# Order of work in a fused convolution stage: opening tiles, a scale factor and a spectrum's mean change places

## The chip, the cores and the metric

The kernel runs on one core of one Trainium2 chip. TensorE (PE) does matrix products, VectorE (DVE) and ScalarE (ACT) elementwise work, GpSimd (POOL) elementwise work and DMA requests, SyncE (SP) DMA requests. PE writes its results to PSUM; the other data live in SBUF (on chip) and in device memory. The metric is the device time of one execution in microseconds, the median of several runs. In all data here the type is 32-bit float.

## The reference

The input x has shape 8 x 32 x 256 x 256 (batch, channel, height, width). Four layers follow one another, each of the form x + layer(groupnorm(x)), with 16 groups of two channels:

```
x = x + spectral(gn(x))      # rfft2, 32 x 32 low modes and 32 x 32 high modes mixed over channels, irfft2, bias
x = x + conv5x5(gn(x))       # one 5 x 5 kernel, the same for every channel, padding 2
x = x + gru(gn(x))           # a recurrence over the 256 columns
x = x + mix(gn(x))           # cumulative maxima in four directions, 1x1 mixing over 5*32 channels
```

Only the second half of the first layer (from modes back to the image) and the second layer matter here; both are in one stage.

## The kernel before

**Stages.** `forward_and_mix` computes the modes and mixes them over channels. `inverse_and_conv` transforms back, adds the input, and applies the convolution layer. `recurrence` and `maxima_and_mix` are the last two layers. The change is in `inverse_and_conv` alone, which is the stage from 355 to 1054 us of the profile.

**Tiling of the convolution stage.** There are 16 units `u`: a batch item and half of its channels (16), taken as two chunks `ch` of 8. A chunk has four groups `g` of two channels, so a unit has eight group convolutions, `g` from 0 to 7 in the main loop ("first" to "eighth group" in the text; `conv(u, g // G, g % G, between)`). The width is cut into nine blocks of 28 columns with a margin on each side; a block's transform is `transform(u, p)`, p from 0 to 8. Even units begin a batch item, odd ones end it.

**The order** is written out by hand (`manual_schedule`): every engine executes its instructions in the order in which the program emits them. One turn of the main loop emits a group convolution of unit u, then work for the next units: `transform(u + 1, p)` (one block; in the fourth group one more inside the convolution, `between`); in groups 4 to 7 `over_rows(u + 2, ...)`, which prepares the unit after next; at the eighth group `transform(u + 2, 0)`, "the lone transform", and `scale(u + 1, 0, 3)`.

**A group convolution** (`conv`, line 487) multiplies x by banded 64 x 64 matrices. Its result lies in three PSUM tiles, the banks: blocks 0 and 1 (first bank, 256 columns), blocks 2 to 5 (middle, 512), blocks 6 to 8 (last, 384). Each bank gets three kinds of tiles: kind 0 opens the accumulation, kinds 1 and 2 add to it, and each kind is a pair of 64 x 64 matmuls, one per half of the rows. The array has four 64 x 64 quadrants. A pair occupies two of them: the diagonal ones for kind 0 of the first and last bank and kinds 1 and 2 of the middle bank, the crossing ones for the rest. Pairs on different quadrants can run at the same time. Kind 0 and kind 1 of one bank lie on different quadrants but add to the same PSUM, so kind 1 waits for a semaphore that the bank's second opening matmul increments:

```
if kind == 1 and i == 0:
    ins._wait_ge(sems[bank], count[0])
```

The banks take turns in four PSUM buffers (`tag="vp", bufs=4`), three per convolution: the first bank gets the buffer that the last bank of the convolution before the previous one had, the middle bank that of the previous first bank, the last bank that of the previous middle bank.

**Eviction** (line 520): VectorE scales the PSUM results by r, adds x in place and sums, in five instructions: blocks 0, 1, then two for the middle bank, one for the last.

**Transform** (line 418, `up`; adds on line 427): 16 matmul passes in 64 x 32 tiles, then two VectorE additions. `over_rows` (line 401, `tp`) is preceding work, 8 passes, whose result ScalarE copies out of PSUM (line 408). **scale** (lines 451, 455, 457): PE sums squares (v), VectorE adds epsilon (ve), GpSimd takes the power -1/2 (r), which line 520 needs. The squares come from ScalarE (line 444). **spectrum** (lines 358 to 372): for a new batch item, one small matmul (y, line 360) and seven small VectorE operations fix the mean in the spectrum and write the group means. `over_rows`, `scale`, `spectrum` and `statistics` share one PSUM buffer, the tag "st". The spectrum is requested (`load_spectrum`) on ScalarE's queue in the third group of an odd unit; of the 8 batch items, the items 2 to 7 are prepared so, in units 1, 3, ..., 11. `store` requests the write of a finished chunk on SP's queue, after the fourth and eighth group; `load` requests the input on POOL's queue.

## Time and profile before

| what | value |
| --- | --- |
| median of 3 runs | 3101.18 us (3096.61 to 3104.53) |
| profiled execution | 3099.62 us, span 3097.8 us |
| PE busy, whole span | 2827.9 us (91%) |
| VectorE, ScalarE, POOL busy | 2584.2 (83%), 1868.6 (60%), 859.9 us (28%) |
| convolution stage, 355 to 1054 us | PE 683.9 of 699.0, VectorE 543.3, ScalarE 465.8 us; DMA engines 69% busy |
| convolution matmuls (line 487) | 4608 passes, 460.6 us busy |
| one eviction: 128, 384, 512 columns | about 0.35, 0.62, 0.75 us, and 0.08 us each to read the sum |

A profile row names the engine, the line of the kernel, the operation, and "output<-inputs" by the program's tile names: vp is the convolution's PSUM, up and tp that of the transforms, v that of scale, y that of spectrum, tt the copy of tp, junk the output of a sum of squares. PE is matmuls, PEld weight loads, which can overlap them. An f32 matmul appears as two passes, each with a weight load. "<-" with a name in a bracket or a list of waits is what ended an engine's idle time. The starts of single passes come from the single records of the trace; the ends of matmuls in it are modelled.

### The profile page before, as it was taken

The numbers are of one execution on the slowest core, as the hardware profiler recorded it, in microseconds if no ns is written. First come the engines' busy times: TensorE is split into PE (matmuls) and PEld (weight loads), VectorE is DVE, ScalarE is ACT, GpSimd is POOL, SyncE is SP. The second block draws the span as 40 slices with busy tenths as digits, with TensorE's granted clock in tenths as the row PEclk, the third lists the DMA queues.
The fourth block names the chain that finished last, engine by engine and source line by source line (L and its number), as shares of the span: only waits on it lengthen the run. The fifth ranks groups of instructions, "written<-read, shape, count | busy, mean of one in ns | idle before, by whom it ended". The sixth has DMA issues, their size and how long they took to land.

```text
span 3097.8 us, 111686 instructions
## 1 busy us (share of the span) xinstructions
PE 2827.9 (91%) x47736; PEld 1625.9 (52%) x47736; DVE 2584.2 (83%) x5178; ACT 1868.6 (60%) x4482; POOL 859.9 (28%) x1247
## 2 busy tenths in 40 slices
PE   7986799999999699999999999999999588888887
PEld 4656244444444366666666666666666333333333
DVE  5753577777777589999999999999999799999997
ACT  3332376667667678888888888888888222222222
POOL 0110011111111255555555555555555300000000
PEclk9985899999999899999999999999999799998998
DMA  9976577777775736656666656666664688888885
GB/s 385 389 278 210 161 226 213 211 210 219 210 215 175 179 91 160 165 143 143 143 150 165 161 142 143 144 155 165 152 146 115 192 319 328 330 322 328 326 327 228
DMA packets 468193, 655.69 MB, mean 212 GB/s; under 512 B 328784, under 2 KB 329696, under 8 KB 441456
## 3 DMA queue, kind: packets, MB, share of 16 engines
q1 hardware_dynamic: 407528, 487.89, 54.1%
q0 software_dynamic: 16784, 84.11, 8.2%
q10 hardware_dynamic: 43384, 76.55, 6.9%
q8 instruction: 374, 6.13, 0.8%
q14 instruction: 123, 1.01, 0.1%
HBM read 371.63 MB, written 272.63 MB: 208 GB/s over the span
## 4 chain that ended last, share of the span: by engine, by line
PE 71%; DVE 20%; DMA 3%; issue 3%; ACT 1%; SPq 0%; POOL 0%; ACTq 0%; DVEq 0%; POOLq 0%
PE vp L487 14%; PE r L753 14%; PE z L753 13%; PE ni L753 6%; PE nh L753 6%; PE up L418 4%; DVE rv L1012 4%; PE yp L131 3%; DVE dq L1018 2%; DVE uq L1020 2%; DVE m L1026 2%; DVE m L1022 2%; DVE m L1024 2%; PE tp L401 2%; PE o L1043 2%
## 5 line engine op out<-in xcount | busy, mean ns | idle before, releaser
L761 PE MATMUL z<-hs,weights 64*64 64x256 f32 x4080 | 539.3, 382 | 0.0
L761 PE MATMUL r<-hs,weights 64*64 64x256 f32 x4080 | 525.0, 375 | 0.0
L761 PE MATMUL ni<-hs,weights 64*64 64x256 f32 x4080 | 524.9, 375 | 0.0
L843 POOL TENSOR_TENSOR xw<-xw,hs 128x256 f32<-128x256 f32 x496 | 339.5, 685 | 635.6 <-DVE hs L842 635.6
L487 PE MATMUL vp<-x,c_conv 64*64 64x512 f32 (+5 forms) x4608 | 460.6, 495 | 4.3 <-DVE x L520 4.3
L1058 ACT ACTIVATE ot<-o,bres 128x512 f32<-128x512 f32 x256 | 154.9, 688 | 505.4 <-PE o L1043 490.0
L520 DVE SCALAR_TENSOR_TENSOR x<-vp,r,x 128x128 f32<-128x128 f32 (+2 forms) x640 | 350.4, 562 | 125.6 <-PE vp L487 106.7
L837 POOL TENSOR_TENSOR a<-zm,xn 128x256 f32<-128x256 f32 x510 | 372.4, 730 | 6.3 <-ACT zm L830 6.1
L835 ACT ACTIVATE n<-n,bih 128x256 f32<-128x256 f32 x510 | 259.2, 508 | 186.3 <-DVE n L834 186.3
L1043 PE MATMUL o<-m,wsc 32*32 32x512 f32 x3072 | 228.6, 724 | 108.1 <-DVE m L1026 104.5
L753 PE MATMUL r<-hs,weights 64*64 64x256 f32 x2040 | 319.1, 389 | 5.0 <-DVE hs L842 4.1
L487 PEld LDWEIGHTS vp<-x,c_conv 64*64 64x64 f32 x4608 | 201.9, 133 | 227.7 <-issue 107.1
L753 PE MATMUL z<-xn,weights 64*64 64x256 f32 x2040 | 305.5, 376 | 14.4 <-ACT xn L733 14.4
L753 PE MATMUL r<-xn,weights 64*64 64x256 f32 x2040 | 305.5, 376 | 1.2 <-ACT rs L828 1.2
L753 PE MATMUL nh<-xn,weights 64*64 64x256 f32 x2040 | 305.7, 377 | 0.0
L753 PE MATMUL z<-hs,weights 64*64 64x256 f32 x2040 | 305.2, 376 | 0.0
L753 PE MATMUL ni<-hs,weights 64*64 64x256 f32 x2040 | 305.2, 376 | 0.0
L733 ACT ACTIVATE xn<-xw,shift,turned 128x256 f32<-128x256 f32 x496 | 290.6, 586 | 0.0
L761 PEld LDWEIGHTS ni<-hs,weights 64*64 64x64 f32 x4080 | 284.5, 133 | 0.3
L829 DVE SCALAR_TENSOR_TENSOR n<-nh,bhh,rs 128x256 f32<-128x256 f32 x510 | 246.3, 483 | 45.9 <-ACT rs L828 31.4
L761 PEld LDWEIGHTS r<-hs,weights 64*64 64x64 f32 x4080 | 280.9, 131 | 0.2
L828 ACT ACTIVATE rs<-r,brz 128x256 f32<-128x256 f32 x510 | 241.3, 473 | 53.9 <-PE r L761 32.5
(162 smaller groups left out, 6233.8 us busy)
## 6 DMA issues: line engine op xcount, KB each, us to landing
xb<-in_xl_dram POOLq DMA_DIRECT2D x96, 768.0 KB, 6.3
xa<-in_xt_dram SPq DMA_DIRECT2D x64, 1024.0 KB
x<-x3d SPq DMA_DIRECT2D x32, 2048.0 KB
fw<-fwd SPq DMA_DIRECT2D x32, 2048.0 KB
out_dram<-ot ACTq DMA_DIRECT2D x64, 1024.0 KB
xw<-x2d SPq DMA_DIRECT2D x248, 256.0 KB
fwd<-fm SPq DMA_DIRECT2D x248, 256.0 KB
x3d<-xw SPq DMA_DIRECT2D x248, 256.0 KB
```

What stands on the lines that cost most here:

```text
L487: ins = nc.tensor.matmul(vps[bank][to, :, dst], lhsT=k.conv[r, P : P + 64] if kind == 2 else k.conv[r, o], rhs=pair_of(u, ch, g, lo, hi, s ...
L520: nc.vector.scalar_tensor_tensor(x, src[o], r1[rows, g : g + 1], x, ALU.mult, ALU.add, accum_out=s1[rows, 0, n, ch, g : g + 1])
L733: nc.scalar.activation(norms[bi][:, b, w], raws[bi][:, b, w], AF.Identity, bias=shift[:, b : b + 1], scale=sc[:, 1, b : b + 1])
L753: ins = nc.tensor.matmul(out[r], lhsT=weights[r, kind, gate, :], rhs=src[r], start=start, stop=stop)
L761: ins = nc.tensor.matmul(out[pairs[1 - i]], lhsT=weights[r, kind, gate, :], rhs=prev[r, :, q0 : q0 + Q], start=False, stop=stop,)
L828: rs = nc.scalar.activation(r, p["r"], AF.Sigmoid, bias=brz[:, 0:1])
L829: nc.vector.scalar_tensor_tensor(m, p["nh"], bhh[:, 2:3], r, ALU.add, ALU.mult)
L835: nc.scalar.activation(m, m, AF.Tanh, bias=bih[:, 2:3])
L837: product = nc.gpsimd.tensor_tensor(a, zm, cur, ALU.mult)
L843: nc.gpsimd.tensor_tensor(raw, raw, new, ALU.add)
L1043: nc.tensor.matmul(pts[b2][i][32 * j : 32 * j + 32].rearrange("p (w q) -> p w q", q=Q), lhsT=wsc[q, b2, t, :], rhs=src[j][q, b2], start=first,
L1058: nc.scalar.activation(ot[:, i], pts[b2][i], AF.Identity, bias=bres[:, b2, i : i + 1])
```

## The change

Three things in `inverse_and_conv` change places; no instruction is added or removed.

1. In `conv`, the first bank's opening tiles are emitted ahead of the middle bank's, in every group convolution.
2. In the eighth group, `scale(u + 1, 0, 3)` is emitted ahead of `transform(u + 2, 0)`.
3. In odd units, `spectrum` of the next batch item is emitted at the end of the sixth group, not of the eighth.

```diff
             count[0] += 1
-            for bank, kind in ((1, 0), (0, 0), (2, 0), (0, 1), (1, 1), (0, 2)):
+            for bank, kind in ((0, 0), (1, 0), (2, 0), (0, 1), (1, 1), (0, 2)):
                 tiles(bank, kind)
...
                     if g < len(PLACES) and more:
                         transform(u + 1, PLACES[g])
+                    if g == 2 * G - 1 and more:
+                        scale(u + 1, 0, 3)
                     if g == 2 * G - 1 and beyond:
                         transform(u + 2, 0)
-                    if g == 2 * G - 1 and more:
-                        scale(u + 1, 0, 3)
...
                     if u % 2 and u + 3 < n:
                         if g == 2:
                             load_spectrum(units[u + 3][0])
-                        elif g == 7:
+                        elif g == 5:
                             spectrum(units[u + 3][0])
```

## The prediction

> **What bounds the kernel now.** I read the page first. Its chain of waits says which engine the end hangs on, and which lines the change can reach there.

> ```profile
> PE 71%; DVE 20%; DMA 3%; issue 3%; ACT 1%; SPq 0%; POOL 0%; ACTq 0%; DVEq 0%; POOLq 0%
> ...
> L487 PE MATMUL vp<-x,c_conv 64*64 64x512 f32 (+5 forms) x4608 | 460.6, 495 | 4.3 <-DVE x L520 4.3
> ```

> All three edits lie in the convolution stage, 355 to 1054 us. There TensorE (PE) is busy 683.9 of 699.0 us, so only what shortens PE's own sequence can help. "Busy" does not say that all parts of the array work, so next comes the list of waits of that stage (waiting engine, line, what it waited for, us, times, longest):

> ```profile
> PEld vp L487 <- PE vp L487: 67.0, 121, 0.9
> ...
> DVE x L520 <- POOL r L457: 10.8, 9, 1.2
> PEld up L418 <- DVE x L427: 8.8, 15, 0.6
> ...
> PEld y L360 <- DVE ve L455: 8.7, 6, 1.4
> ...
> PE vp L487 <- DVE x L520: 4.3, 7, 1.0
> ```

> The first line is the large one: in 121 of 128 group convolutions the weight loads stop for 0.56 us on PE's own earlier matmuls. The fifth: six times, once in each odd unit that has a spectrum to prepare, the y matmul waits for VectorE. Where the first wait sits is seen in the timeline of the weight loads (start, length; in brackets the idle time before):

> ```profile
> 706.81 0.64 PEld L487 LDWEIGHTS vp<-x,c_conv 64*64 64x64 f32 x12 [0.38 <-issue]
> 708.01 1.07 PEld L487 LDWEIGHTS vp<-x,c_conv 64*64 64x64 f32 x20 [0.56 <-PE vp L487]
> ```

> Twelve loads are the opening tiles of all three banks. Then nothing until 1.20 us after the start, when the first bank's crossing tiles begin.

> **Why 1.20.** Each f32 matmul is two passes. From the single records of this convolution, counted from its start at 706.81: first bank (256 columns, diagonal quadrants) second pass from 0.29, recorded end 0.66; middle bank (512, crossing quadrants) second pass from 0.49, recorded end 1.08; last bank (384, diagonal) second pass from 0.82. The tiles that resume at 1.20 wait for the *first* bank's signal, 0.54 after its own end but 0.13 after the end of the *middle* bank, which stands ahead of it in the program. The first convolution of the stage, at a lower granted clock, separates the two readings: first bank ends 356.73, middle bank 357.57, loads resume 357.70. That is again 0.13 after the middle bank, but 0.97 after the first. So the signal comes out in program order, and the shortest bank's signal is held by the longest's.

> [...] the 64x32 tiles of the up matmuls start about 0.09 us after the last 64x64 pass has streamed. So both quadrant pairs must finish before a transform starts.

> **Part 1, the order of opening tiles.** Nothing is added or removed; no DMA moves. With the first bank in front, its signal is seen at 0.66 + 0.13 = 0.79. Passes on one quadrant follow each other by 0.21 (256 columns), 0.32 (384) and 0.42 to 0.43 us (504, 512). The crossing quadrants are free at 0.49 + 0.43 = 0.92; weights asked for at 0.79 take 0.13 (LDWEIGHTS, 133 ns), also 0.92. Left on them: two tiles of the first bank and two of the last, 4 x 0.215 + 4 x 0.32 = 2.14 us, to 3.06. Today they run from 1.20 (plus 0.05 cold start) to 3.40. The diagonal side gains nothing: the middle bank's next tile needs that bank's own signal at 1.20 as before and its side ends at 2.98, so it is not the later one. Gain per convolution up to 0.335 us; the second crossing tile is now queued behind the middle bank's loads at 1.21, which may cost up to 0.08. I take 0.30, from 0.22 to 0.335.

> How often: of 128, the 15 fourth groups (a transform inside) gain nothing[...]. The first group of unit 0 is split likewise. The last unit's convolutions follow each other directly and run in a loop of 4.28 us through VectorE: third bank's opening, middle bank's end, its two evictions (0.75 + 0.08 us each), third bank again. The order leaves that loop alone. 104 remain: **104 x 0.30 = 31.2 us**. Units 14 and 15 have ScalarE just ahead of PE (a variance matmul at 1025.82 already waits 0.35 us for it), where I take back 1.0.

> Does VectorE follow? Its middle-bank evictions end 4.64 us after a convolution's start (705.93 against 701.29). The next third bank opens at 3.19 + 1.02 (up) + 0.29 = 4.50, at worst delayed to about 4.8, that is 0.6 into its convolution. What follows it in program order starts at 0.79 at the earliest, so 0.2 us of cover remain. If it fails, it costs at most 0.3 in the one gap per unit with only an up between (about 4 us in all).

> **Parts 2 and 3, the unit boundary.** The timelines of PE, and of ScalarE, at an odd boundary:

> ```profile
> 710.30 1.09 PE L418 MATMUL up<-tt,c_gw 64*32 64x512 f32 x16
> 711.32 0.83 PE L451 MATMUL v<-sq,c_valid 128*128 128x4 f32 x6
> 713.51 0.41 PE L360 MATMUL y<-spec,c_dc 128*128 128x32 f32 x2 [1.36 <-DVE ve L455]
> 713.86 3.56 PE L487 MATMUL vp<-x,c_conv 64*64 64x512 f32 x36
> ```

> ```profile
> 708.01 0.56 ACT L408 COPY tt<-tp 128x512 f32<-128x512 f32 x1
> ...
> 709.99 0.19 ACT L444 ACTIVATION_READ_ACCUMULATOR junk<-x 128x1 f32 x1
> ```

> The y matmul shares the single "st" PSUM buffer with the variance matmul, whose reader ve is queued on VectorE behind five evictions and two adds. Moving the mean to the sixth group removes 713.86 - 712.09 = 1.77 us per odd boundary (v gives way to the next convolution after 0.77 at an even one, 667.73 to 668.50). In the sixth group y follows an over_rows, and waits for ScalarE's copy of that one's PSUM instead. There this copy starts 0.05 after the matmuls and ends at 701.996, 0.70 after the next convolution now starts (701.293); plus 0.08 to be seen and 0.35 for y: 1.13 us. Queued behind y is convolution 7, and through it VectorE's evictions. **6 x (1.77 - 1.13) = 3.8 us.** The mean's seven VectorE operations (1.88 us from 713.49 to 715.37) fall into VectorE's gap ahead of those evictions, 1.32 us today and 1.13 longer; uncovered, they would delay evictions by 1.9 us. Its DMAs do not move: the spectrum is still requested in the third group, and its last packet of the slowest load ran at 695.1, against first use after 701.

> Scale ahead of the lone transform: the same six v matmuls and ve, and POOL's power (1.47 us) earlier by the two adds (1.28 us). That would end VectorE's 10.8 us of waits for r at even boundaries. Today PE does not idle for these, so they count nothing; with shorter convolutions r would have been late, and the move keeps it level. No queue entry of POOL or SP is passed: that transform issues no load. Its price: v's last pair needs ScalarE's sums of tile 8, which end 8.88 us after convolution 7's start at even boundaries (666.59 - 657.71), 8.98 when seen. PE reaches the pair at 9.01 - 2 x 0.30 + 0.46 = 8.87. Wait 0.11, 8 boundaries without a mean (even ones and unit 13): 0.9 us. Were all v's held, 0.57 each, 4.6 us. At odd boundaries y's 1.13 us cover it. The lone transform's adds come 0.15 later; nobody waits for them before the second group.

> **Sum.** 31.2 - 1.0 + 3.8 - 0.9 = 33.1 us. Profiled execution: 3099.6 us, span 3097.8, so 3066.5 and 3064.7. The median of the runs is 1.6 above that execution: 3101.2 - 33.1 = 3068.1, **3068 us**.

> **Rivals.** *Half the gain (0.10).* The recorded ends are modelled. Were the first bank's signal seen 0.15 later than I take, each convolution gains 0.15: 104 x 0.15 + 2 = 17.6, 3084 us. For: nobody waits for that signal alone today. Against: 0.13 after a recorded end fits at two clocks.
> *No gain (0.10).* The loads at 1.20 are in truth held by the middle bank's wait, 13 ns behind in the same burst. Then parts 2 and 3 alone remain, 2 us, 3099. Against: the loads held are ahead of that wait in the program.
> *Slower (0.08).* The middle bank, with the longest tiles, starts its opening late, now that it is second: its signal gates the diagonal side. From 0.42 us later (3.40 - 2.98) it decides. If it had to await the first bank's signal (0.79), 0.37 lost 104 times, less 2: 36.5 us, 3138. Against: openings on different quadrants start within 20 ns in every record, and its PSUM buffer, released by the first bank's evictions 2.93 us after the previous start, is free.

> **How the numbers follow.** The likeliest case has 0.72, and by its ends (0.22 and 0.335 per convolution, 0 to 5 us at the boundaries) lies between 3060 and 3080. A difference of under 0.3% (9.3 us) can't be told from none. Faster: 0.72 + 0.10 = 0.82; same 0.10; slower 0.08. The range takes in the half case: 3056 to 3090.

> **What would show it.** The 0.56 us gap of the weight loads on PE's own vp shrinks to about 0.2 or splits in two; a convolution from start to the next up takes 3.19 instead of 3.49, in the fourth groups unchanged; the stage (355 to 1054) is 33 us shorter, the others the same; y idles about 0.8 us in the sixth group and the boundary's 1.36 is gone; r no longer holds VectorE. The prediction is wrong if the gap stays at 1.20 us, or if a wait on VectorE or ScalarE of like size stands in its place.

## The result, and the profile after

The changed kernel takes 3070.26 us (median of 6 runs, 3066.26 to 3074.67), the kernel before 3105.06 us in the 6 runs that count with them (3096.61 to 3106.54). The ratio is 0.9896, with a 95% interval of 0.9883 to 0.9908. The forecast was 3068 us; its own base was the first three runs, 3101.18. The profiled execution took 3069.0 us, span 3067.2.

From the page of the changed kernel, the chain of waits and the convolution's row:

```profile
PE 69%; DVE 20%; DMA 5%; issue 3%; ACT 2%; SPq 0%; ACTq 0%; POOL 0%; DVEq 0%; POOLq 0%
...
L487 PE MATMUL vp<-x,c_conv 64*64 64x384 f32 (+5 forms) x4608 | 428.8, 491 | 4.9 <-DVE x L520 4.9
```

The convolution's matmuls are busy for 428.8 us in place of 460.6: 31.8 us gone with the same 4608 passes. DMA's share of the chain is up from 3% to 5%, which the forecast did not expect.

The waits of the stage, here 355 to 1021 us (waiting engine, line, what for, us, times, longest):

```profile
DVE spec L358 <- DMA spec<-smd: 14.0, 3, 4.7
...
PEld tp L401 <- DVE yb L362: 7.6, 3, 2.6
...
PEld y L360 <- ACT tt L408: 6.8, 6, 1.1
...
PE vp L487 <- DVE x L520: 4.9, 10, 0.6
PE tp L401 <- DVE yb L362: 4.9, 3, 1.7
PE y L360 <- ACT tt L408: 4.1, 6, 0.7
...
DVE x L520 <- POOL r L457: 1.1, 1, 1.1
```

PE's wait for its own vp (67.0 us, 121 times) is no longer in the list; I had expected about 0.2 us of the gap to stay; the single records show 0.09. VectorE's wait for r fell from 10.8 to 1.1 us. y now waits for ScalarE's copy, as forecast. New are the first two lines: three times VectorE waits for the *spectrum's load*, and PE's over_rows behind it.

The timeline of the weight loads at the end of unit 6 (start, length, idle time before):

```profile
647.72 2.24 PEld L487 LDWEIGHTS vp<-x,c_conv 64*64 64x64 f32 x34 [0.39 <-issue]
650.15 0.14 PEld L487 LDWEIGHTS vp<-x,c_conv 64*64 64x64 f32 x2 [0.18 <-issue]
650.88 0.89 PEld L451 LDWEIGHTS v<-sq,c_valid 128*128 128x128 f32 x6 [0.59 <-ACT junk L444]
651.79 0.18 PEld L418 LDWEIGHTS up<-tt,c_gw 64*32 64x32 f32 x16
```

Where twelve loads, a hole of 0.56 us and twenty loads stood, 34 come in one run. The convolution reaches what follows 3.16 us after its start (650.88 - 647.72) and not 3.49.

To see where each part went, I compare the starts of all 128 convolutions in the two traces and write down by how much each step from one to the next grew (us; columns are groups 1 to 8; the 128th step ends with the last eviction):

```
unit 2   -1.87 -0.33 -0.33 -0.06 -0.33 -0.33 -0.33 -0.19
unit 3   -0.33 -0.33 -0.33 -0.06 -0.33 +0.77 +1.36 -0.59
unit 4   -0.33 -0.33 -0.33 -0.06 -0.33 -0.33 -0.33 -0.19
unit 9   -0.33 -0.33 -0.33 -0.06 -0.33 +0.77 -0.33 -2.11
all 128 steps: -27.97
```

Units are counted from 0 here, as u is in the code. Units 4 and 9 are the patterns of an even and an odd unit; 3, 5 and 7 are alike; units 0, 14 and 15 differ and are taken up below. From this table: -0.33 per convolution; the even boundary gives back 0.14 (-0.19), the sixth group with y costs 1.10 (+0.77), its boundary saves 1.78 (-2.11). In units 3, 5 and 7 the seventh group is 1.69 worse than in unit 9 and the boundary 1.52 worse.

### The profile page after: what moved, and what is told of

It is laid out like the page before. It is cut to its first block, busy times and chain, and to the rows that moved or that the text cites. A ratio compares the mean times of both kernels' runs of the same rounds, so it can differ in the third digit from the quotient of the medians.

```text
span 3067.2 us, 111686 instructions
## 1 busy us (share of the span) xinstructions
PE 2796.5 (91%) x47736; PEld 1645.3 (54%) x47736; DVE 2585.2 (84%) x5178; ACT 1870.4 (61%) x4482; POOL 858.2 (28%) x1247
## 4 chain that ended last, share of the span: by engine, by line
PE 69%; DVE 20%; DMA 5%; issue 3%; ACT 2%; SPq 0%; ACTq 0%; POOL 0%; DVEq 0%; POOLq 0%
PE r L753 14%; PE z L753 13%; PE vp L487 11%; PE ni L753 6%; PE nh L753 6%; PE up L418 4%; DVE rv L1012 4%; PE yp L131 3%; DMA spec<-smd 3%; DVE dq L1018 2%; DVE uq L1020 2%; DVE m L1026 2%; DVE m L1024 2%; DVE m L1022 2%; PE sp L158 2%
## 5 line engine op out<-in xcount | busy, mean ns | idle before, releaser
L487 PE MATMUL vp<-x,c_conv 64*64 64x384 f32 (+5 forms) x4608 | 428.8, 491 | 4.9 <-DVE x L520 4.9
L520 DVE SCALAR_TENSOR_TENSOR x<-vp,r,x 128x128 f32<-128x128 f32 (+2 forms) x640 | 350.6, 563 | 87.9 <-PE vp L487 75.1
L487 PEld LDWEIGHTS vp<-x,c_conv 64*64 64x64 f32 x4608 | 222.4, 132 | 180.0 <-issue 104.4
```

The lines of the kernel that those rows point to most:

```text
L487: ins = nc.tensor.matmul(vps[bank][to, :, dst], lhsT=k.conv[r, P : P + 64] if kind == 2 else k.conv[r, o], rhs=pair_of(u, ch, g, lo, hi, s ...
L520: nc.vector.scalar_tensor_tensor(x, src[o], r1[rows, g : g + 1], x, ALU.mult, ALU.add, accum_out=s1[rows, 0, n, ch, g : g + 1])
```

## The experiments

**1. The order alone.**

```diff
-            for bank, kind in ((1, 0), (0, 0), (2, 0), (0, 1), (1, 1), (0, 2)):
+            for bank, kind in ((0, 0), (1, 0), (2, 0), (0, 1), (1, 1), (0, 2)):
```

> Only the opening order is changed; scale and the spectrum's mean stay where they were. If the first bank's signal is given out in program order (my theory): nearly every group convolution 0.33 us shorter, 104 x 0.33 = 34 us, less what VectorE loses by a late r at the unit boundaries (0.2 to 0.6 us at 8 or 9 of them, 2 to 5 us); the 1.36 us wait of y at odd boundaries stays. Ratio to the kernel before about 0.990. If the gain of the whole change came from the boundaries (rival): no change, ratio 1.000.

Measured: 3081.74 against 3101.03 us, ratio 0.9935 (0.9919 to 0.9951). The convolutions are 0.33 us shorter, exactly as in the whole change, so this edit carries the gain. But in the trace the stage is only 11.1 us shorter. The late r costs what was expected: behind the eight boundaries without a mean the second group gains next to nothing, a loss of about 0.36 us each and 2.9 us in all that is gone in run 2, with scale ahead. Most of the loss has another cause. Three odd boundaries grew by 4.7, 4.4 and 3.1 us, and four convolutions after odd boundaries ran 1.4 to 2.1 us longer than their neighbours (such convolutions of run 9 had a granted clock of 0.51, or of 0.71 with the transform behind counted in; see the end). VectorE's timeline at the first of the three:

```profile
440.21 0.69 DVE L427 TENSOR_TENSOR x<-up,xb 128x512 f32<-128x512 f32 x1
445.37 0.69 DVE L427 TENSOR_TENSOR x<-up,xb 128x512 f32<-128x512 f32 x1 [4.47 <-DMA x2d<-x]
445.98 0.15 DVE L455 TENSOR_SCALAR ve<-v 128x4 f32<-128x4 f32 x1
```

The lone transform's second add (the other two boundaries look alike) writes into the buffer of the unit's first chunk, whose store (x2d) has not ended. ve is queued behind it, y waits for ve's PSUM, and PE stands still for 6.20 us. At the old pace the store had ended in time.

**2. Order and scale, the mean left in the eighth group.**

```diff
-                        elif g == 5:
+                        elif g == 7:
                             spectrum(units[u + 3][0])
```

> The whole change but for the mean, which stays in the eighth group. My theory: against the whole change it loses 6 x (1.77 - 1.10) = 4 us of saved boundary waits, but regains the three units in which the mean waited for the spectrum's late load, about 3.2 us each, 9.6 us. So about 5 us faster than the whole change, ratio to the kernel before about 0.988; r does not hold VectorE. If the late load costs nothing in the end (rival): about 4 us slower than the whole change, 0.991.

Measured: 3072.57 us, ratio 0.9905 (0.9879 to 0.9930), too wide to tell from the whole change. In its trace the stage is 32.9 us shorter than before, 4.9 more than in the whole change. That this meets the expected 5 is luck. The 9.6 us of the late load are regained, as expected. But the 4 us at the boundaries are not lost: odd boundaries are -1.25 in place of -2.11 and the second group after them -0.20 in place of -0.33, together 1.0 us, and there is no y in the sixth group, which costs 1.10. And one convolution (unit 8, second group) grew by 4.90 us. The lone transform's second add waited 4.15 us ahead of it; the profile names PE's transform as what it waited for, but that had long ended, and the wait ends with the signal of a DMA, by its place the first chunk's store. PE stopped for 2.81 us for the evictions behind the add, and the 5.0 us that follow ran at a granted clock of 0.66. So the move of the mean gains nothing here, even where the load is in time.

**3. The two moves alone**, with the old opening order.

```diff
-            for bank, kind in ((0, 0), (1, 0), (2, 0), (0, 1), (1, 1), (0, 2)):
+            for bank, kind in ((1, 0), (0, 0), (2, 0), (0, 1), (1, 1), (0, 2)):
```

> The old opening order with both moves (scale ahead, mean in the sixth group). My theory: 6 x (1.77 - 1.10) = 4 us faster, ratio 0.9987, the spectrum's load in time at the old pace, v never waiting. Rival, that the moves carry the gain: 30 us faster, 0.990.

Measured: 3092.23 us, ratio 0.9973 (0.9964 to 0.9982). The trace has +1.10 in six sixth groups, -1.77 at six boundaries and nothing anywhere else but -1.54 after the first odd boundary, 5.6 us in all. The 1.10 and 1.77 are those expected; the gain of 8.8 us in the runs is larger than the 4 of the forecast. The 1.54 is a convolution of the kernel before at a granted clock of 0.64 over 3.6 us (see the end). That such losses vary from run to run and make up the rest was not tested.

**4. The first bank's crossing tiles ahead of the middle bank's second**, old opening order.

```diff
-            for bank, kind in ((1, 0), (0, 0), (2, 0), (0, 1), (1, 1), (0, 2)):
+            for bank, kind in ((1, 0), (0, 0), (2, 0), (0, 1), (0, 2), (1, 1)):
```

> The old opening order (middle bank first), and both crossing tiles of the first bank emitted ahead of the middle bank's second tile. If the first bank's signal itself is held behind the middle bank's (my theory): the loads still resume 1.20 us after a convolution's start, and a convolution still takes 3.49 us to the next transform. If the loads were held by the middle bank's wait, which now stands behind them (rival): they resume at about 0.8 us and a convolution takes about 3.2 us, 31 us less in all.

Measured: 3100.21 us in its one run, no change. The timeline of the weight loads:

```profile
706.89 0.64 PEld L487 LDWEIGHTS vp<-x,c_conv 64*64 64x64 f32 x12 [0.39 <-issue]
708.09 1.08 PEld L487 LDWEIGHTS vp<-x,c_conv 64*64 64x64 f32 x20 [0.56 <-PE vp L487]
```

The hole is the same 0.56 us, though the instruction that waits for the middle bank now stands behind both of the first bank's crossing tiles and no longer right behind the first. In the single records the first bank's load resumes at 1.201 us and that of the middle bank at 1.231. This rules out the "no gain" rival: what the loads wait for until 1.20 is the first bank's own signal.

**5. The new order with the old release**: the first bank's crossing tile waits for the middle bank's signal.

```diff
-                    ins._wait_ge(sems[bank], count[0])
+                    ins._wait_ge(sems[max(bank, 1)], count[0])
```

> The whole change, but the first bank's crossing tile waits for the middle bank's signal in place of its own. My theory: the order of emission does nothing by itself, only the earlier release does, so the loads resume 1.20 us after the start again, a convolution takes 3.49 us, and what is left is that of the two moves, about 5 us under the kernel before. If the order itself packs the quadrants better (rival): still about 3.16 us per convolution.

Measured: 3086.83 us in one run; in its trace the stage is 10.9 us shorter than before, not the expected 5. The timeline of its weight loads:

```profile
699.46 0.63 PEld L487 LDWEIGHTS vp<-x,c_conv 64*64 64x64 f32 x12 [0.39 <-issue]
700.62 1.06 PEld L487 LDWEIGHTS vp<-x,c_conv 64*64 64x64 f32 x20 [0.53 <-PE vp L487]
```

The hole is back at 0.53 us (resuming 1.16 after the start, not 1.20), and a convolution gains 0.05 in place of 0.33. The order of emission therefore does little by itself; the earlier release does nearly all. The other 0.05 is most of what exceeds the expected 5. The loads resume 0.07 us after the middle bank's recorded end, where in the kernel before it was 0.13; why stays open.

**6. The spectrum's load moved**: requested on SP's queue behind the even unit's last store, three groups earlier in the program.

```diff
-            queue = nc.scalar if b > 1 else nc.sync
+            queue = nc.sync
...
                         store(u, g // G)
+                    if u % 2 == 0 and u + 4 < n and g == 7:
+                        load_spectrum(units[u + 4][0])
```

and the request in the third group of odd units taken out.

> The whole change, with the next spectrum's load requested on SP's queue behind the store that ends the even unit before, not on ScalarE's queue in the third group of the odd unit. If the late load cost the whole change three units of about 3.2 us: the three go, about 9 us faster than the whole change, ratio to the kernel before about 0.987, the sixth group +0.77 and the boundary -2.11 in all six odd units. Rival, that the stores that now share the queue take the load's place as the late transfer: no gain, or a wait of VectorE for a store in the lone transform's adds.

Measured: 3062.69 us, ratio 0.9877 (0.9857 to 0.9897). In the trace all six odd units have +0.77 and -2.11, as expected, and the stage is 35.3 us shorter than before, 7.4 better than the whole change. The load is not faster here: it takes 15 to 20 us. SP's queue issues the store first, so the request comes only some 3.5 us earlier than in the whole change, 20.2 to 20.9 us ahead of the use in place of 16.9. That is just enough; in unit 7 VectorE still waits 0.55 us for it. And the rival's store appeared once: after unit 7 the lone transform's second add waited 3.11 us until a DMA's signal, and the convolution behind it (unit 8, second group) grew by 1.93 where the others shrank by 0.33. This is what is missing from the 9.6 us of the late loads.

**7. And y in another PSUM buffer**: the "up" ring of three in place of "st".

```diff
-            y0 = ps.tile([P, C], F32, name=f"y0_{b}", tag="st")
+            y0 = ps.tile([P, C], F32, name=f"y0_{b}", tag=tag, bufs=bufs)
...
+                        spectrum(units[u + 3][0], "up", 3)
```

> As the run before, and the mean's y matmul has its PSUM in the up tag's ring of three, whose next slot was evicted long before, so that it need not wait for ScalarE's copy. Theory: the sixth group of six odd units loses 0.35 us for y and not 1.10, so 6 x 0.75 = 4.5 us less than the run before, ratio about 0.9855. Rival: the ring's shift makes the next transform wait for two adds of the last one, and what is saved comes back as a wait of up on VectorE.

Measured: 3059.91 us, ratio 0.9879 (0.9852 to 0.9907). PE's timeline has no wait ahead of y:

```profile
677.45 1.08 PE L401 MATMUL tp<-c_eh,spec 128*64 128x256 f32 x8
678.46 0.41 PE L360 MATMUL y<-spec,c_dc 128*128 128x32 f32 x2
```

The sixth group stands at +0.01 to +0.02, so y costs 0.34 to 0.35 and not 1.10, and no wait of up grew to match. The stage is 41.7 us shorter than before, 6.4 more than in run 6. Of these, y brings 6 x 0.76 = 4.6 us, as expected; 2.3 are run 6's wait for a store, which this execution does not have. The trace shows the gain of y; the ratios of the two runs overlap.

**8. The whole change again**, without an edit.

> The whole change once more on this chip, for comparison with the two runs beside it: ratio 0.990, and whether the same three units (third, fifth and seventh) have the late spectrum. If how late it is depends on how the transfers happen to meet, other units or another number.

Measured: 3069.27 us, ratio 0.9905 (0.9880 to 0.9930). In this execution the load was late in four units (1, 5, 7 and 9), mostly by less, and the stage is 32.2 us shorter than before. Which loads are late, and how late, differs between executions of the same kernel. By the packets in the traces, the six loads took (us; in brackets the run):

```
                   request to last packet              request to use
before             7.8  9.5  8.3 11.1  9.0  8.5        29.5
order alone (1)   21.1  8.5 12.2 11.7 20.1 19.5        27.6 or more
order, scale (2)   9.6  9.7 18.8 21.4 10.6 10.4        27.3 or more
moves alone (3)    9.0  8.6  8.5 15.6  8.7  7.9        18.4
old release (5)    8.6  9.4  9.0  8.4  9.7  8.4        18.2
load on SP (6)    15.4 18.3 18.5 19.9 18.6 19.3        20.2 to 20.9
whole change      10.4 21.2 20.8 21.1 10.6 13.0        16.9, or when it lands
whole change (8)  18.6  8.6 18.5 20.8 19.1 13.4        16.9, or when it lands
whole change (11) 12.5 20.5 21.0 20.8 20.8  9.9        16.9, or when it lands
```

Of the loads on ScalarE's queue, one of 18 took over 15 us at or near the old pace (kernel before, runs 3 and 5), and 16 of 30 at the new one. In units 1 and 3 of the whole change the store's first request comes 5.9 us after the load's, in units 1 and 7 of the kernel before 7.1 us. This alone does not decide it, as unit 1's load took only 10.4. Late stores go with slow loads: the three boundaries that grew in run 1 (units 1, 9 and 11) are those with a load of about 20 us, and run 2's late store is that of unit 7, whose load took 21.4. Which holds up the other, and what part the input loads on POOL's queue have, was not separated.

**9. The new order alone, with the load on SP's queue** as in run 6.

> The new opening order alone, as in the first experiment, but with the spectrum's load requested on SP's queue at the end of the even unit. If what the first experiment lost at odd boundaries (up to 5 us each) was the load slowing the store of the unit's first chunk, for which the lone transform's adds wait: these losses go, an odd boundary is within 0.3 us of the kernel before, and the stage is about 30 us shorter than before and not 11. Rival, that y, queued behind late evictions at the faster pace, is the cause: the losses stay.

Measured: 3080.18 us in one run, the stage 21.8 us shorter. All odd boundaries with a mean are at -0.06, but for unit 7's +0.16; the losses of run 1 there are gone. Less than the expected 30 remain since four convolutions after odd boundaries took 1.7 to 2.9 us longer than their neighbours, 8 us in all; the granted clock was 0.51 over one of them, and 0.71 over each of two with the transform behind it (see the end). One of them is slow in the kernel before too, so the table of steps hides it.

**10 and 11. More rounds** for the version of run 7 and for the whole change.

> The version with the load on SP's queue and y in the up ring, once more with more rounds, beside the whole change: ratio to the kernel before 0.986, about 12 us faster than the whole change.

> The whole change with more rounds on the same chip: ratio 0.990.

Measured: 3065.43 us, ratio 0.9884 (0.9868 to 0.9901), and 3072.82 us, ratio 0.9903 (0.9889 to 0.9918). The version of run 7 is ahead in both comparisons by 7 to 9 us of the medians, less than the 12 expected; the intervals overlap. In the trace of run 11 the load was late in four units (3, 5, 7 and 9) and the stage is 25.5 us shorter than before. The trace of run 10 has two waits of the lone transform's adds for a store:

```profile
DVE x L427 <- DMA x2d<-x: 8.1, 2, 4.9
```

The convolutions that follow are longer by 2.3 and 4.0 us, and the stage is 6 us longer than in run 7. This is what run 6's rival named: with the spectrum out of the way, the first chunk's store is the next transfer that is just in time, as in run 6 once.

## Why the prediction was right or wrong

**The bound and the release: right.** The hole was the first bank's signal, held behind the middle bank's. Run 4 excludes the other reading and run 5 brings the hole back with one semaphore. I expected the crossing quadrants to resume at 0.92 us; a record of the changed kernel (unit 9, eighth group) has 0.92. The loads come at 0.72 where I had 0.79, since the signal is seen 0.07 after the recorded end and not 0.13; this gains nothing, as the quadrants are free only at 0.92. The second crossing tile, whose queueing I had priced at up to 0.08, starts at 1.36, straight behind the first (1.15 + 0.21). The term was mis-sized only by that: 0.33 in place of 0.30 per convolution.

**Which convolutions: right but for two units.** The fourth groups gained 0.06 where I had put nothing (the transform inside starts 2.16 us after the convolution and not 2.22), and the last unit next to nothing. Unit 14 gained 1.2 us where other even units gained 2.2, and of the loss about half is ScalarE's, as I had it: 0.48 at the boundary, where v waits for it. The rest is in groups 5 to 7: the first of them gains nothing, and the other two now take 4.28 us each, the period of the last unit's loop through VectorE. In unit 0 I left out the first group alone, but its first five together gained nothing; why was not looked into.

**The boundaries: the sum right, the split between the moves wrong.** y in the sixth group 1.10 (expected 1.13; y starts 0.05 us after the end of ScalarE's copy, where I had 0.08), the odd boundary 1.78 (1.77), v's wait at even boundaries 0.14 (0.11). r no longer holds VectorE. But I booked the 1.77 to the mean's move and no gain to scale's. Runs 1 and 2 differ by scale alone: an undisturbed odd boundary goes from -0.06 to -1.25, and y's wait there from 1.63 to 0.29 us, since the ve that it waits for no longer stands behind two adds. With scale ahead, the mean's move saves 0.86 at the boundary and 0.13 in the second group after it, and costs 1.10: it pays only where y does not wait for ScalarE's copy, as in run 7. The rival that the middle bank starts late is out: its opening passes start 0.01 us after the first bank's in the same record.

**The spectrum's load: wrong.** The step that failed reads: "Its DMAs do not move ... its last packet of the slowest load ran at 695.1, against first use after 701." I took the load's own time as fixed, 11.1 us at most. At the new pace the first chunk's store is requested 5.9 us after the load and not 7.1 (units 1 and 3 here, 1 and 7 before; run 8 shows that this alone does not decide it), and three of six loads took 21 us, against a use that the two edits had brought from 29.5 to 16.9 us behind the request. VectorE's timeline in unit 7 of the changed kernel:

```profile
683.93 1.28 DVE L427 TENSOR_TENSOR x<-up,xb 128x512 f32<-128x512 f32 x2
689.85 0.69 DVE L358 TENSOR_SCALAR spec<-spec 64x1024 f32<-64x1024 f32 x1 [4.64 <-DMA spec<-smd]
690.58 0.19 DVE L362 TENSOR_TENSOR yb<-y,bias 128x32 f32<-128x32 f32 x1
```

and PE's:

```profile
690.82 1.08 PE L401 MATMUL tp<-c_eh,spec 128*64 128x256 f32 x8 [1.59 <-DVE yb L362]
691.84 1.66 PE L487 MATMUL vp<-x,c_conv 64*64 64x256 f32 x8
693.99 2.56 PE L487 MATMUL vp<-x,c_conv 64*64 64x384 f32 x28 [0.49 <-DVE x L520]
```

VectorE's evictions stand behind the waiting instruction, the next over_rows needs y's PSUM, and the convolution needs the evicted buffers. Per late unit 1.69 + 1.52 = 3.2 us, three units 9.6 us. In run 6 the load is requested early enough, and the loss is gone.

**The sum.** In the profiled execution, with the units and boundaries taken from the table: boundaries -1.78 x 6 + 1.10 x 6 + 0.14 x 8 = -3.0; late loads +9.6; one slow clock of the kernel before that is gone, -1.5; the rest, which is the order, -33.1. Together -28.0. My sum was -33.1: order 30.2, boundaries 2.9, no late load. Two misses, 2.9 more from the order and 9.6 lost to the load, partly cancelled, and the first stage happened to end 4 us sooner in this execution (the first convolution starts at 351.6, not 355.6; 357.5 in run 8 of the same kernel). Nothing in the change touches that stage. So the total came out nearer than the terms, by luck.

## What to carry to other kernels

In these traces the loads that wait for a short producer's signal resumed at 1.20 us with it behind a long one in the program, and at 0.72 with it ahead. Where several producers run side by side, try the shortest first, and look for holes in the weight loads even where PE reads as fully busy. A gain on the bounding engine can bring a transfer closer to its use and to the next transfer at once (here from 18.4 us between request and use in run 3 to 16.9); for each load and store that is now in time, compare its slack with the pace after the change, not before. When two moves serve the same wait, price each with the other in place: here scale's move had already taken most of what the mean's was to bring. When a step is moved to where a buffer is shared, ask which release it will meet there; another ring with a long-free slot made y's wait vanish.

## What the runs showed of the hardware

```profile
700.50:701.10 0.60, 0.57 (x3) 0.51 (x3) 0.59 (x1) 0.60 (x1) 0.47 (x1) 0.50 0.81 318
701.10:707.19 6.09, 6.09 (x38) 2.97 (x37) 2.02 (x12) 5.77 (x14) 1.00 (x1) 0.51 0.76 194
```

That convolution took 6.1 us where its neighbours take 3.16. Behind the boundaries after units 3 and 9, the convolution and the transform behind it ran 5.80 us at a clock of 0.71:

```profile
529.60:535.40 5.80, 5.80 (x53) 2.70 (x53) 3.02 (x14) 5.61 (x13) 1.16 (x1) 0.71 0.77 208
788.90:794.70 5.80, 5.80 (x53) 2.79 (x52) 3.03 (x14) 5.61 (x13) 1.18 (x1) 0.71 0.70 190
```

The kernel before has such a place too, after its first odd boundary, 1.54 us longer at a clock of 0.64 over 3.6 us:

```profile
445.40:449.00 3.60, 3.60 (x30) 1.99 (x33) 1.52 (x8) 3.51 (x7) 1.29 (x1) 0.64 0.75 188
```

Of the six stops of 1.63 us in run 9, four had a longer convolution behind them. Of the six of 1.36 us in the kernel before, one had a lower clock behind it, and of the three of 1.59 to 1.65 us that the late load caused in the whole change, none: there the clock stayed at 1.00 from 355 to 1021 us. In run 2 a stop of 2.81 us was followed by 5.0 us at 0.66. What decides it was not shown.

Matmuls of different quadrants ran at the same time, and their starts did not all keep the order of emission. In the kernel before, the opening passes of the first and middle bank start within 0.02 us of each other in 123 of the 128 convolutions (not in all, as the forecast had it: in five of the last unit they are 0.11 to 0.32 us apart). In the convolution at 706.81 the first bank's second pass starts at 0.29 us, 0.20 ahead of that of the middle bank (0.49), which precedes it in the program; yet the loads that wait for its signal resume only at 1.20, after the middle bank's recorded end at 1.08. In the changed kernel (unit 9, eighth group) they come at 0.72, ahead of that end, which is again at 1.08.
